# Half of the additions of a softmax denominator as accumulating transfers issued by GpSimd

## The chip, the cores and the metric

The kernel runs on one NeuronCore of a Trainium2 chip. The metric is the time of one execution on the device in microseconds (us), lower being better. Engines are named as in the profile: PE is TensorE (matmuls), PEld its weight loads, DVE is VectorE, ACT is ScalarE, POOL is GpSimd, SP is SyncE, which here only issues transfers.

## The reference

The input x is 8 images of 512 channels by 32 x 32 pixels, float32. Two residual layers follow each other. Layer 1 is a depthwise 3 x 3 convolution, a pruning and a 1 x 1 convolution. Layer 0 holds what the change touches: a 1 x 1 convolution to 2 x 256 channels, then twice (l = 0, 1) a block of a 3 x 3 convolution, an attention over all 1024 pixels and a 1 x 1 convolution, and at the end a 1 x 1 convolution over everything collected. The attention, cut to what matters:

```python
q, k, v = (qkv[:, 0], qkv[:, 1], qkv[:, 2])            # 4 heads of 64 channels, 1024 pixels
logits = jnp.einsum("bhdi,bhdj->bhij", q, k + r) * HD ** (-0.5)
a = jax.nn.softmax(logits, axis=-1)                    # over j
out = jnp.einsum("bhij,bhdj->bhdi", a, v)
```

Softmax needs, for each head and each pixel i, the sum of exp(logits) over the 1024 pixels j.

## The kernel before, in words

**Order of the work.** Images follow each other. Each function adds its pieces to a list under a short name (`add`), and `go` takes them from these lists in the order of a plan, a text of such names: `FIRST` for image 0, `HEAD` and then `TAIL` for images 1 to 6, `HEAD` and then `LAST` for image 7. The two attentions of an image lie in `FIRST` or in `HEAD`. The wrapper `InOrder` keeps that order on PE, DVE, ACT and SP; GpSimd runs its instructions in the order in which they are written too. So each engine has one queue, in the order of the plan, and an instruction that waits holds up everything behind it on its engine. The plans were made by a planner, which is not part of the file.

**One attention** (`attention()`, lines 971 to 1073) has 32 steps: 2 pairs of heads (m), 2 halves of the pixels i (ih), and 8 tiles of 128 pixels j (jt, innermost). The pieces of a step s are

- `s`, scores: 4 small matmuls (8 in the profile, which counts two instructions for each float32 matmul) into a PSUM tile `ps_s` of which there are two;
- `e`, exponentials: ACT writes exp of 128 x 1024 scores to a fresh work tile `e`;
- `w`, values: 4 matmuls of `e` with v, added up over jt in two PSUM banks `ps_av` from a pool of three;
- `p`, add_up: DVE adds `e` to the running tile `sum` of the group (m, ih). The first addition of a group takes two `e` tiles, so 7 additions serve 8 steps.

After the 8 steps of a group, `h` (ACT) copies one bank, and `z` (DVE) adds the other to it, which frees the banks for the next group. After the two groups of one m, `n` multiplies the two `sum` tiles by ones (`ps_dn`, PE), `nr` takes reciprocals (4 pieces on DVE), `ns` spreads them over the partitions by two transfers, and `sc` (DVE) scales z with them. Only then can `m`, the matmuls of the next convolution (`ps_m`), start. The other names that come up below are `Q` (pieces of the last convolution of an image), `o` and `O` (products of the last 1 x 1 convolution of the image before, with `ot` before them and `fr`, `f` behind), `t`, `l`, `lr`, `lp` (its depthwise convolution, activation and pruning; `lp` has an instruction on GpSimd).

**Work tiles.** All `e`, `sum` and many other tiles of 128 x 1024 float32 come from one pool of `NWORK = 11` tiles, used in turn. A tile is given out again when everything that read or wrote it is done; the first writer of its next use waits for that.

The lines that carry the accumulation before the change:

```python
def add_up(s):
    m, ih, jt = steps[s]
    if jt == 1:
        sm[m, ih] = work_tile("sum").rearrange("p (a n) -> p a n", a=2)
    t = flat(sm[m, ih])
    nc.vector.tensor_tensor(t, flat(es[s - 1]) if jt == 1 else t, flat(es[s]), ALU.add)
```

Of the kernel before, what the change touches and what calls it, by code (L numbers as in the profile page):

```python
# [15 lines left out]
P = 128  # L16
# [9 lines left out]
V_N = 396  # L26
LIMIT = 1e20
PITCH = F // 4 + 1
NWORK = 11
NRING = 5  # L30

FIRST_PARTS = [
# [10 lines left out]


FIRST = """
    g*6 gm gd gv g gp g gb gm gd ga gv ga c gp fo gb c ta0 ga ta0 ga ta0 ti0 fo ta2 to0*2 c
    ti0*2 ca ta2*2 c rl ca ta1*3 ti2 ti1 to1 d ti1 d y ya to1 ti1 y ya ti2 to2 d y ti2 d to2 rl
    ya y d*2 ya d P Rc R P d*3 Rc R d*2 P Rc R B P Rc R B*2 P*2 Rc R E Ez B Rc R E Ez k*2 X k dw
    ta0 ka k kp ka ta0*2 v kp ti0 v va ti0 v ti0 q v va ta1 q ta1 qa q*2 qa ta1 s e s e p to0 s
    e p w to0 s e w*2 ti1 s e p ti1*2 p s e p w s to1 s e p w e p w s w to1 ta2 e s e w h p z  # L50
    ta2 s e p ta2 s ti2 e w*2 s e w ti2 to2 ti2 s e w s e to2 w s e w s e w s e rh p w p*5 h z
    s*2 w e*2 n s e w p s p w nr e p w nr*2 s e nc s nr e ns p w s e p w*2 nc s e p w h z s e s
    w s*2 p*2 e w p e*2 p sc p w sc s w e p w s e p w*3 h z n nr*4 ns nc sc Q K m ma sc dp mr
    m*2 ma mr m ma mr ma mr d*4 Q nc K d*3 P d P Rc R d*2 Rc R d*2 P Rc R P*2 Rc B R B P Rc R E
    Ez Rc B*2 R E Ez k X dx k*3 ka*2 kp*2 v*2 q v*2 va*2 cw*3 rk cw q*2 qa q qa s*2 e*2 p s e p
    w s e w s p cw*2 e s e w s e p rk p w s e p*2 s e w s e g*2 w*2 p w h z s e w cw s e p*2
    cw*2 rk s e w*2 s e w s*2 p e rk w p s e g w p g p s*2 e g w g e*2 p w h z p s w e g p w n
    nr s e nr p w g s e s p w nr e s e w p w*2 s nr p e s e w h ns p s e p nc*2 s w e p w s e p
    w s e p w s sc e p s e p w sc w*3 h z n nr*2 Q nr*2 ns z Q sc*2 nc m*2 ma mr ma mr m ma nc m
    ma mr gm mr gd Q gv u A Q x u i A x i gp i*2 Q gb ga*4 Q im id Q iv A Q x ip i*2 ib b bm t*3  # L60
    Q A t x i*2
"""

HEAD = """
    t c*2 t b im id bm c ca iv t ip t l t*2 ib lr b t*3 c bm ca b y d y bm d ya d*2 ya d*3 y P d
    Rc R d*2 P Rc R d P ya d kd Rc R B P Rc R P B*2 Rc R E P Ez Rc B R E Ez y k*3 ya k ka t X lp
    ka t*4 v*2 l t va v*2 va t lr q*2 t*2 lp t q qa s e q qa s e p s t e w t p s e w l p s*2 w
    e*2 p w s p e s w t s w t s e*2 p lr e p w*2 h z s e p w s t w s p s e p e*2 w p s w p e w s
    t e p s w s e w e t p*2 w lp t h z s*2 e p e w s*2 n e*2 w p w s nr s p e w nr e p s e w nr
    s nr t p ns l w e p*2 w lr lp w ot h s e s w p ot s w ot s e*2 p*2 e w p s w e w s e p*2 z  # L70
    sc w nc w*2 h n nc o O nr ok Ok sc z nr*3 ns o ou oa O*2 Ou sc m Oa m sc nc m ma m ma mr ma
    ot mr ma mr o nc mr d ou Ou o O d ou Ou o d O ou*2 oa Ou*2 d Oa o O P d*2 Rc d*3 R P kd d*2
    Rc R d P Rc P R B Rc P B Rc P R B*2 Rc R ou E oa Ou R Oa o O dp E Ez*2 X k v*2 k ou oa Ou
    fr*2 Oa ka fr f*2 fr f*2 dx va k v*2 va k q*2 ka q qa q qa s e s*2 e p e w p s e p w s*2 e*2
    p*2 w s*2 e*2 w*2 s g p e w*2 s e w p s*2 h g e g p w s w z p e*2 s w e g*2 s*2 w*2 p e*2 g
    p*3 g s w*2 e p s e w h s*2 e*2 p z p w*2 s p e p s n w nr*3 w e s g e p w p s e p w*2 s nc
    e nr s ns e nc w s h s p w z w e p s e w s p e*2 p sc s w e p*2 w s sc e p w*3 h n nr*4 ns z
"""

TAIL = """  # L80
# [45 lines left out]
def fast_kernel(  # L126
# [158 lines left out]
    def flat(ps):  # L285
        return ps.rearrange("p n f -> p (n f)")
# [20 lines left out]
    def add(name, *pieces):  # L307
        todo.setdefault(name, []).extend(pieces)
# [662 lines left out]
    def attention():  # L971

        last = HW // P - 1
        steps = [(m, ih, jt) for m in range(2) for ih in range(2) for jt in range(HW // P)]
        pss, es, sm, accs, rs, dns, rr, parts = {}, {}, {}, {}, {}, {}, {}, {}
        quarters = [(r, c) for c in range(2) for r in range(2)]

        def half(r):
            return slice(r * HD, (r + 1) * HD)

        def scores(s):
            m, ih, jt = steps[s]
            ps = pss[s] = big_tile("ps_s")
            for a, c in quarters:
                j = jt * P + c * HD
                nc.tensor.matmul(
                    ps[half(c), a, :],  # L990
                    kr[half(a), m, j : j + HD],
                    qy[half(a), m, ih * 512 : (ih + 1) * 512],
                    start=True,
                    stop=True,
                )

        def exponentials(s):
            e = es[s] = work_tile("e").rearrange("p (a n) -> p a n", a=2)
            nc.scalar.activation(flat(e), flat(pss.pop(s)), AF.Exp, scale=HD ** -0.5)

        def add_up(s):
            m, ih, jt = steps[s]
            if jt == 1:
                sm[m, ih] = work_tile("sum").rearrange("p (a n) -> p a n", a=2)
            t = flat(sm[m, ih])
            nc.vector.tensor_tensor(t, flat(es[s - 1]) if jt == 1 else t, flat(es[s]), ALU.add)

        def values(s):
            m, ih, jt = steps[s]
            if jt == 0:  # L1010
                accs[m, ih] = [bank_tile(f"ps_av{r}") for r in range(2)]
            for r, a in quarters:
                h = 2 * m + a
                nc.tensor.matmul(
                    accs[m, ih][r][half(a), :],
                    vt[half(r), jt, h * HD : (h + 1) * HD],
                    es[s][half(r), a, :],
                    start=(jt == 0),
                    stop=(jt == last),
                )  # L1020

        def part(m, ih):
            t = parts[m, ih] = work_tile("part")[:, :512]
            nc.scalar.copy(t, accs[m, ih][1])

        def join(m, ih):
            zz = z[:, m, ih * 512 : (ih + 1) * 512]
            nc.vector.tensor_tensor(zz, accs[m, ih][0], parts[m, ih], ALU.add)

        def sums(m):  # L1030

            dn = dns[m] = ps_mm.tile([P, 512], F32, tag="mm", name="ps_dn")
            for i in range(4):
                t = sm[m, i // 2]
                nc.tensor.matmul(
                    dn[32 * i : 32 * (i + 1), :], ones, t[:, i % 2, :], start=True, stop=True
                )

        def reciprocal(m, q):
            if q == 0:  # L1040
                rr[m] = work_tile("r")
            c = slice(q * 128, (q + 1) * 128)
            nc.vector.reciprocal(rr[m][:, c], dns[m][:, c])

        def spread(m):

            wide = rs[m] = work_tile("rw")
            for ih in range(2):
                twice = rr[m][half(ih), :512].unsqueeze(1).to_broadcast([HD, 2, 512])
                nc.sync.dma_start(wide[:, ih * 512 : (ih + 1) * 512], twice)  # L1050

        def check(m, src):

            n = rng_used[0]
            rng_used[0] += 1
            src = dns[m] if src == 0 else rr[m][:, :512]
            nc.scalar.activation(rr[m][:, 512:], src, AF.Copy, accum_out=rng[:, n : n + 1])

        def scale(m, ih):
            c = slice(ih * 512, (ih + 1) * 512)  # L1060
            nc.vector.tensor_tensor(z[:, m, c], z[:, m, c], rs[m][:, c], ALU.mult)

        both = [(m, ih) for m in range(2) for ih in range(2)]
        n = len(steps)
        add("s", *[lambda s=s: scores(s) for s in range(n)])
        add("e", *[lambda s=s: exponentials(s) for s in range(n)])
        add("p", *[lambda s=s: add_up(s) for s in range(n) if steps[s][2]])
        add("w", *[lambda s=s: values(s) for s in range(n)])
        add("h", *[lambda m=m, ih=ih: part(m, ih) for m, ih in both])
        add("z", *[lambda m=m, ih=ih: join(m, ih) for m, ih in both])  # L1070
        add("n", *[lambda m=m: sums(m) for m in range(2)])
        add("nr", *[lambda m=m, q=q: reciprocal(m, q) for m in range(2) for q in range(4)])
        add("ns", *[lambda m=m: spread(m) for m in range(2)])
        add("nc", *[lambda m=m, i=i: check(m, i) for m in range(2) for i in range(2)])
        add("sc", *[lambda m=m, ih=ih: scale(m, ih) for m, ih in both])
# [799 lines left out]
```

## Time and profile before

| | before |
|---|---|
| time, median of 2 runs | 2598.15 us (2598.12 to 2598.18) |
| span of the profiled execution | 2595.2 us, granted TensorE clock 0.998 |
| PE busy | 2558.3 us, 99% of the span |
| DVE busy | 2084.2 us, 80% |
| ACT busy | 1185.6 us, 46% |
| POOL busy | 98.0 us, 4% |
| additions of exponentials on DVE | 448 instructions, 553.5 us |
| transfers | 268.49 MB, mean 103 GB/s |

The profile shows one execution. A busy share is an average over the span. The trace shows for each instruction when it started, and what it waited for; matmuls are pipelined, their ends are modelled, so the distance from one start to the next tells more of PE than its busy time.

### The profile page before, as it was taken

Reading aid. Unit: us, or ns where it says so; the run is one execution under the profiler, and the core shown is the slowest. Engines: PE = TensorE matmul, PEld = TensorE weight load, DVE = VectorE, ACT = ScalarE, POOL = GpSimd, SP = SyncE. Lnnn points to the kernel's source line nnn. Section 1 sums busy time; section 2 is a strip of 40 time slices with the busy share of each in tenths; the row PEclk is TensorE's granted clock in tenths of the full one; section 3 lists DMA queues with packets and bytes.
Section 4 is the critical chain, followed back from the end, with each engine's and each line's share of the span. In section 5 each row is a group of like instructions: output and inputs, shape, how many; then the busy total and the mean of one; then the engine's idle time right before and its main releaser. Section 6 shows DMA issues by size and latency. Waiting matters only on the chain.

```text
span 2595.2 us, 36342 instructions
## 1 busy us (share of the span) xinstructions
PE 2558.3 (99%) x14806; PEld 1291.6 (50%) x14806; DVE 2084.2 (80%) x2982; ACT 1185.6 (46%) x1523; POOL 98.0 (4%) x71
## 2 busy tenths in 40 slices
PE   8999999999999999999999999999999999999997
PEld 5454463634636346463464635545355554645443
DVE  8887589877898878887788778887788877888657
ACT  3635436353462544635445344444445444353534
POOL 1000000000000000000000000000000000000000
PEclk9999999999999999999999999999999999999999
DMA  9445230522305113060130602306121151302300
GB/s 349 154 155 203 67 121 25 188 76 73 113 27 213 51 65 122 17 247 17 65 122 17 248 17 80 107 18 246 33 98 73 61 204 33 138 35 96 110 17 34
DMA packets 81773, 268.49 MB, mean 103 GB/s; under 512 B 6848, under 2 KB 37312, under 8 KB 65600
## 3 DMA queue, kind: packets, MB, share of 16 engines
q1 hardware_dynamic: 78048, 262.69, 28.5%
q10 hardware_dynamic: 3552, 3.41, 0.4%
q8 instruction: 118, 1.93, 0.3%
q14 instruction: 55, 0.45, 0.1%
HBM read 212.34 MB, written 36.96 MB: 96 GB/s over the span
## 4 chain that ended last, share of the span: by engine, by line
PE 92%; DVE 4%; ACT 2%; DMA 1%; issue 0%; ACTq 0%; POOL 0%; SPq 0%; DVEq 0%
PE ps_av L105 16%; PE ps_s L105 16%; PE ps_c L105 12%; PE ps_cv L105 11%; PE ps_qk L105 8%; PE ps_cv2q L105 8%; PE ps_q L105 6%; PE ps_v L105 4%; PE ps_m L105 4%; PE ps_y L105 4%; PE ps_dn L105 1%; ACT qy L105 1%; DVE ht L105 1%; DVE vtmp L105 0%; DVE mid L105 0%
## 5 line engine op out<-in xcount | busy, mean ns | idle before, releaser
L105 ACT ACTIVATE e<-ps_s 128x1024 f32<-128x1024 f32 x512 | 509.7, 1023 | 287.1 <-PE ps_s L105 267.4
L105 PE MATMUL ps_s<-qy,kr 64*64 64x512 f32 x4096 | 513.6, 592 | 1.4
L105 DVE TENSOR_TENSOR sum<-sum,e 128x1024 f32<-128x1024 f32 x384 | 475.4, 1238 | 40.2 <-ACT e L105 21.1
L105 PE MATMUL ps_av<-e,vt 64*64 64x512 f32 x4096 | 506.4, 590 | 0.0
L105 DVE SCALAR_TENSOR_TENSOR ht<-xn,v_sb,ht 128x961 f32<-128x961 f32 (+1 forms) x256 | 312.2, 1227 | 8.3 <-ACT ht L105 5.0
L105 PEld LDWEIGHTS ps_s<-qy,kr 64*64 64x64 f32 x4096 | 160.6, 132 | 288.7 <-issue 185.2
L105 PEld LDWEIGHTS ps_av<-e,vt 64*64 64x64 f32 x4096 | 165.8, 133 | 276.9 <-issue 267.6
L105 PE MATMUL ps_qk<-z,wring 128*128 128x512 f32 x512 | 229.7, 596 | 2.0 <-ACT z L105 1.3
L105 DVE TENSOR_TENSOR sum<-e 128x1024 f32<-128x1024 f32 x64 | 78.1, 1221 | 126.2 <-ACT e L105 124.9
L105 ACT COPY c<-ps_c 128x256 f32<-128x256 f32 x96 | 35.6, 370 | 263.4 <-PE ps_c L105 260.2
L105 PEld LDWEIGHTS ps_qk<-z,wring 128*128 128x128 f32 x512 | 95.8, 190 | 118.1 <-issue 99.9
L105 DVE RECIPROCAL r<-ps_dn 128x128 f32<-128x128 f32 x128 | 112.8, 923 | 11.3 <-PE ps_dn L105 9.0
L105 PEld LDWEIGHTS ps_c<-kr,wring 128*128 128x128 f32 x1024 | 116.8, 192 | 8.0 <-issue 7.7
L105 PE MATMUL ps_c<-vt,wring 128*128 128x128 f32 x1024 | 118.1, 276 | 1.8 <-DMA wring<-u 1.1
L105 PE MATMUL ps_c<-qy,wring 128*128 128x128 f32 x1024 | 117.6, 275 | 0.9 <-ACT c L105 0.5
L105 PEld LDWEIGHTS ps_c<-vt,wring 128*128 128x128 f32 x1024 | 116.2, 192 | 2.6 <-ACT c L105 2.1
L105 PE MATMUL ps_cv<-pt,w_sb 128*128 128x512 f32 x256 | 117.3, 609 | 0.0
L105 PE MATMUL ps_c<-kr,wring 128*128 128x128 f32 x1024 | 117.0, 275 | 0.0
L105 PEld LDWEIGHTS ps_c<-qy,wring 128*128 128x128 f32 x1024 | 115.8, 192 | 1.3 <-ACT c L105 0.7
L105 PE MATMUL ps_v<-wring,z 128*128 128x256 f32 x512 | 114.8, 379 | 0.7 <-DVE kr L105 0.7
L105 PE MATMUL ps_m<-z,wm_sb 128*128 128x512 f32 x256 | 112.5, 592 | 0.0
L105 PE MATMUL ps_y<-pt,w_sb 128*128 128x512 f32 x256 | 112.3, 592 | 0.0
(177 smaller groups left out, 3231.2 us busy)
## 6 DMA issues: line engine op xcount, KB each, us to landing
wring<-u SPq DMA_DIRECT2D x96, 1024.0 KB, 4.8
pt<-in_x SPq DMA_DIRECT2D x32, 512.0 KB, 9.6
rw<-r SPq DMA_DIRECT2D x64, 256.0 KB, 3.4
xt<-in_x SPq DMA_DIRECT2D x32, 512.0 KB, 5.9
out<-xt SPq DMA_DIRECT2D x32, 512.0 KB, 3.2
kr<-r SPq DMA_DIRECT2D x14, 1024.0 KB, 6.9
wring<-q SPq DMA_DIRECT2D x14, 896.0 KB, 5.6
wring<-in_wqkv SPq DMA_DIRECT2D x16, 768.0 KB, 4.8
```

Source lines behind the costliest of these rows:

```text
L105: made = method(*args, **kwargs)
```

## The change

Of each attention's 32 steps, the first 28 are taken in pairs (s, s + 1) with s even. For a pair, a new piece `pd` has GpSimd issue a transfer that adds the tile `e` of step s + 1 onto the tile `e` of step s in SBUF; DVE then adds only the even tile to `sum`. The last four steps (28 to 31) are left with one addition each on DVE. So there are 14 transfers and 14 additions in an attention in place of 28 additions. It is for taking half of these additions from DVE. The transfer overwrites tile s, so it waits until `w` of step s has read it, and until `e` of step s + 1 is written. As tiles are held longer, the work pool gets 14 tiles in place of 11[...]. The plans `FIRST` and `HEAD` are new as a whole; `TAIL` and `LAST` are unchanged.

The core of the diff:

```diff
-NWORK = 11
+NWORK = 14
...
+        paired = [s for s in range(0, len(steps), 2) if s < len(steps) - 4]
+        rest = [s for s in range(len(steps)) if s % 2 == 0 or s - 1 not in paired]
+
+        def add_pair(s):
+            nc.gpsimd.dma_start(flat(es[s]), flat(es[s + 1]), accum_op=ALU.add)
+
         def add_up(s):
             m, ih, jt = steps[s]
-            if jt == 1:
+            if jt == 2:
                 sm[m, ih] = work_tile("sum").rearrange("p (a n) -> p a n", a=2)
             t = flat(sm[m, ih])
-            nc.vector.tensor_tensor(t, flat(es[s - 1]) if jt == 1 else t, flat(es[s]), ALU.add)
+            nc.vector.tensor_tensor(t, flat(es[s - 2]) if jt == 2 else t, flat(es[s]), ALU.add)
...
-        add("p", *[lambda s=s: add_up(s) for s in range(n) if steps[s][2]])
+        add("pd", *[lambda s=s: add_pair(s) for s in paired])
+        add("p", *[lambda s=s: add_up(s) for s in rest if steps[s][2]])
...
-    nc = bacc.Bacc("TRN2", target_bir_lowering=False, num_devices=1)
+    nc = bacc.Bacc("TRN2", target_bir_lowering=False, num_devices=1, dynamic_dma_scratch_size=2048)
```

The ends of the attentions in the plans, each up to `n` and a little beyond (old line first, new line second). First attention of `HEAD`, second attention of `HEAD` (there the plan ends), first and second attention of `FIRST`:

```diff
-s w p ot s w ot s e*2 p*2 e w p s w e w s e p*2 z sc w nc w*2 h n nc o O nr ok Ok sc z nr*3 ns
+w p s pd ot e*2 s w pd s e p w s e*2 z sc p*5 w nc w*2 h o n nc O nr ok Ok z nr*3 ns
...
-w z w e p s e w s p e*2 p sc s w e p*2 w s sc e p w*3 h n nr*4 ns z
+w e w*2 p z pd s e s sc s w pd e*2 p e w s sc p e p*4 w*3 h n nr*4 ns z
...
-s w e p w s e p w*3 h z n nr*4 ns nc sc Q K m
+s pd p*3 e p w*2 s e w p w*2 h z Q n nr*4 ns sc nc K m
...
-s sc e p s e p w sc w*3 h z n nr*2 Q nr*2 ns z Q sc*2 nc m*2
+s sc e s e w sc w p*5 w*2 h z Q n nr*4 ns z Q sc*2 nc m*2
```

## The prediction, made before the run

> **What bounds the kernel now.** First the page: busy shares, and the chain of work that ended last.
>
> ```profile
> PE 2558.3 (99%) x14806; PEld 1291.6 (50%) x14806; DVE 2084.2 (80%) x2982; ACT 1185.6 (46%) x1523; POOL 98.0 (4%) x71
> PE 92%; DVE 4%; ACT 2%; DMA 1%; issue 0%; ACTq 0%; POOL 0%; SPq 0%; DVEq 0%
> ```
>
> PE is the limit, and DVE, which the change relieves, is not. Busy PE could still be slow PE, so I took the distances between starts from the timeline: 8 small matmuls (one `s` or `w`) take 0.86 us, 0.107 each.
>
> ```profile
> 1040.23 1.04 PE L105 MATMUL ps_s<-qy,kr 64*64 64x512 f32 x8
> 1041.09 1.90 PE L105 MATMUL ps_av<-e,vt 64*64 64x512 f32 x16
> ```
>
> In the same way the chain gives 0.429 us for a 128x512 matmul (16 in 6.87), 0.112 for 128x128 (192 in 21.44), 0.216 for 128x256 (16 in 3.45). With the counts of the groups: 8192 x 0.107 + 2664 x 0.429 + 3072 x 0.112 + 512 x 0.216 = 2474, and some 30 for `ps_dn` and the group sums: PE needs about 2504 us of the 2595. At most 91 us (3.5%) can be won by anything that leaves the matmuls alone. Where are they? Windows over the 317 us of one middle image have PE busy in all but 0.25 us:
>
> ```profile
> sum 317.00, PE 316.75 PEld 160.39 DVE 258.38 ACT 145.41 POOL 10.71; mean PE 18.63 PEld 9.43 DVE 15.20 ACT 8.55 POOL 0.63
> ```
>
> In the list of waits, what PE loses to DVE's additions is 0.4 us in all; its longest wait is in the first 8 us of the kernel. DVE in turn waits in these additions for the exponentials:
>
> ```profile
> PE pm L105 <- DVE mv L105: 9.1, 2, 8.0
> PE ps_dn L105 <- DVE sum L105: 0.4, 1, 0.4
> DVE sum L105 <- ACT e L105: 146.0, 87, 8.9
> ```
>
> So there is next to nothing to win inside an image. What can be lost is read at the ends of the attentions, where PE comes to `n` and needs the sums. First attention of a `HEAD` (DVE, PE), then the second:
>
> ```profile
> 1077.87 6.53 DVE L105 TENSOR_TENSOR sum<-sum,e 128x1024 f32<-128x1024 f32 x5
> 1080.08 1.04 PE L105 MATMUL ps_s<-qy,kr 64*64 64x512 f32 x8
> 1083.62 1.89 PE L105 MATMUL ps_dn<-sum,ones 128*32 128x512 f32 x8
> 1094.12 3.17 PE L105 MATMUL ps_m<-z,wm_sb 128*128 128x512 f32 x7
> 1212.50 1.04 PE L105 MATMUL ps_s<-qy,kr 64*64 64x512 f32 x8
> 1214.66 1.23 DVE L105 TENSOR_TENSOR sum<-sum,e 128x1024 f32<-128x1024 f32 x1 [0.23 <-ACT e L105]
> 1216.04 1.07 PE L105 MATMUL ps_dn<-sum,ones 128*32 128x512 f32 x8
> ```
>
> The last addition ends at 1084.3 and 1215.9, which is 4.2 and 3.4 us after the last `s` (step 31) starts, and `n` follows at once. There is no slack here: whatever delays the last sum delays PE. After the first, `ps_m` comes 10.5 us behind `n` with only 9 us of other matmuls between: reciprocals, `rw` transfer and scaling are on the path too.
>
> [...]
>
> **The change part by part.**
>
> Removed: 14 of 28 additions in each of 16 attentions, 224 x 1.238 us = 277 us of DVE (80% to 70%):
>
> ```profile
> L105 DVE TENSOR_TENSOR sum<-sum,e 128x1024 f32<-128x1024 f32 x384 | 475.4, 1238 | 40.2 <-ACT e L105 21.1
> ```
>
> Worth 0: they lie beside PE, which waited 0.4 us for them.
>
> Added: 224 transfers. The latency L of one, from its last input to the release of DVE, is not in the trace.
>
> ```profile
> wring<-u SPq DMA_DIRECT2D x96, 1024.0 KB, 4.8
> kr<-r SPq DMA_DIRECT2D x14, 1024.0 KB, 6.9
> out<-xt SPq DMA_DIRECT2D x32, 512.0 KB, 3.2
> ```
>
> Low end 3.2 (as a plain copy of the same size); high end 6.9 (the slower 1 MB row[...]). [...] the last two transfers of an attention are issued 1.7 us apart[...]. I take **L = 5.5**.
>
> In mid-attention L is hidden. Walking the new plan with 0.86 us per `s` and `w`, the transfer of pair (4, 5) of the first `HEAD` attention can start 7.7 us before `z`, which the next group's banks need about 1.7 us later; before `z` stand one addition on it and `z` itself, 1.9 us. That holds to L of about 7. Behind a waiting `pd`, GpSimd's queue holds only other `pd`, prunings (1.8 us each, the last due at `ot` some 5 us after its place) and the small powers of the normalizations, which come after the attention. Fourteen tiles give a tile back some 17 to 20 us after it is taken, against e, `w`, L and addition of about 12: hidden.
>
> At the ends it isn't hidden. In both `HEAD` attentions, from the end of `w` of step 26, which releases the last transfer, to the start of step 31's `s` there are 5 pieces on PE, 4.3 us. DVE's queue then holds five additions: that of pair (26, 27), and behind it, in order, steps 28 to 31. They end L + 5 x 1.24 = L + 6.2 after the release, thus L + 1.9 after the last `s` starts. Before it was 4.2 and 3.4. The loss is L - 2.3 in the first attention (the `o` that the plan puts ahead of `n` only moves filler, for the path n to `ps_m` is critical there) and L - 1.5 in the second, where the plan ends and nothing fills: 3.2 + 4.0 = 7.2 us. Seven images run `HEAD`: **50 us**.
>
> `FIRST` puts a `Q` ahead of `n`, which hides the late sums but takes filler from behind `n`. Before:
>
> ```profile
> 142.52 1.04 PE L105 MATMUL ps_s<-qy,kr 64*64 64x512 f32 x8
> 146.06 1.07 PE L105 MATMUL ps_dn<-sum,ones 128*32 128x512 f32 x8
> 154.03 6.17 PE L105 MATMUL ps_m<-z,wm_sb 128*128 128x512 f32 x14
> ```
>
> From the last `s` to `ps_m` 11.5 us, of which n to `ps_m` 8.0. Now `s`, three `w` (3.4), `Q` (16 x 0.43 = 6.9), then the 8.0 with PE empty: 18.3, loss 6.8. In the second attention (s at 266.3, n 270.7, `ps_m` 281.0, 14.7 in all) it becomes 4.3 + 5.2 (`Q`, 12 matmuls) + 8.5 = 18.0, loss 3.3. Together **10 us**.
>
> The new start (a `y` ahead of the `c`): same matmuls, and the second `P` waited for its weights (1.1 us), not for these; 0, +-2. [...] Sum: 7 x (2L - 3.8) + 10 = 14L - 17 = 60 us at L = 5.5: 2598 + 60 = **2658**.
>
> **The rivals.**
>
> A. All hidden: the sums arrive as before because L is near 3 or the release comes earlier than I walk it, and the relieved DVE pays the rest. For it: DVE has 30% free, and only the last transfer matters. Against it: five additions stand behind it. At L = 3.2 the sum is 28 us, 2626; with no loss at all 2598. This one is not slower by over 2%.
>
> B. The transfers are slow[...]. At L = 9 the ends cost 14 x 9 - 17 = 109, and `z` waits at two group ends of an attention, 1.5 us each by the walk above: 16 x 2 x 1.5 = 48. That gives 2755. For it: no adding transfer has been seen here. Against it: [...] DMA is 9 to 24% busy in the four attention windows that I looked at.
>
> C. Faster: DVE's relief removes small stalls. The bound is 91 us[...]; 0.4 us hangs on the sums. At best some 5 us: 2593.
>
> **How the numbers follow.** Forecast [...] 0.62; A 0.22; B 0.14; C 0.02. 2% slower begins at 2650, which is L = 4.9: about 0.7 of the forecast, and B, make 0.57 slower; faster by 2% would need half of all PE slack, 0.01; the rest, 0.42, is within 2%. Range: from 2612, which cuts off half of A and C, to 2705, which cuts off most of B.
>
> **What would show it.** Right: PE waiting in `ps_dn` for `sum`, some 4 us at the second attention of each of seven images, and for `z` before `ps_m`; DVE idle in `sum` waiting for the transfer on `e`; the landing time gives L. An idle gap of about 7 us before `ps_m` near 155 us shows the `FIRST` step. Wrong: `ps_dn` without waits (A), or scores waiting on exponentials and `ps_av` on `z` in mid-attention (B).

## The result, and the profile after

The changed kernel takes 2729.95 us (two runs, 2727.55 to 2732.34) against 2598.15: a ratio of 1.0507, 95% interval 1.0462 to 1.0552. It is slower by 132 us, on the side that was forecast and by more than twice the amount (60 us, range to 2705).

The page of the changed kernel, busy shares, the chain of work that ended last, and what the change added:

```profile
PE 2611.4 (96%) x14806; PEld 1323.7 (48%) x14806; DVE 1825.8 (67%) x2758; ACT 1184.1 (43%) x1523; POOL 288.1 (11%) x295
...
PE 84%; DMA 7%; DVE 6%; ACT 2%; issue 1%; SPq 0%; ACTq 0%; DVEq 0%; POOL 0%; POOLq 0%
...
L1006 POOL DMA_DIRECT2D e<-e x224 | 194.1, 867 | 1235.2 <-ACT e L105 970.9
...
L105 DVE TENSOR_TENSOR sum<-sum,e 128x1024 f32<-128x1024 f32 x160 | 197.7, 1236 | 62.3 <-DMA e<-e 54.9
...
e<-e POOLq DMA_DIRECT2D x224, 512.0 KB, 4.9
```

DVE lost 258 us of work, as meant. None of it shows in the time. PE does the same 14806 matmuls, but busy plus idle changed: idle from 37 to 119 us, and PE's own busy time from 2558 to 2611, so that its matmuls also ran slower. The chain now has 7% of transfers and 6% of DVE in it. The list of waits of the same run (us in total, times, longest) says where PE stood:

```profile
PE ps_dn L105 <- DVE sum L105: 51.6, 16, 4.7
PE ps_s L105 <- ACT e L105: 15.6, 12, 5.6
PE ps_m L105 <- DVE z L105: 7.8, 2, 6.5
...
DVE sum L105 <- DMA e<-e: 370.1, 86, 17.5
```

The 0.4 us that PE waited for sums has become 51.6, at 16 places: both attention ends of images 1 to 7, and in image 0 the `n` in the middle of the first attention and the one at the end of the second. Read one of them, the second attention of an image with `HEAD`, in the timeline. First GpSimd, then DVE, then PE:

```profile
1285.23 0.86 POOL L1006 DMA_DIRECT2D e<-e  x1 [0.86 <-PE ps_av L105]
```
```profile
1291.57 1.23 DVE L105 TENSOR_TENSOR sum<-e 128x1024 f32<-128x1024 f32 x1 [3.05 <-DMA e<-e]
1292.90 3.88 DVE L105 TENSOR_TENSOR sum<-sum,e 128x1024 f32<-128x1024 f32 x3
1297.24 1.23 DVE L105 TENSOR_TENSOR sum<-sum,e 128x1024 f32<-128x1024 f32 x1 [0.46 <-DVE sum L105]
```
```profile
1289.23 1.04 PE L105 MATMUL ps_s<-qy,kr 64*64 64x512 f32 x8
1290.09 2.75 PE L105 MATMUL ps_av<-e,vt 64*64 64x512 f32 x24
1292.77 1.05 PE L105 MATMUL ps_dn<-sum,ones 128*32 128x512 f32 x4
1298.52 1.84 PE L105 MATMUL ps_dn<-sum,ones 128*32 128x512 f32 x4 [4.70 <-DVE sum L105]
...
1311.56 4.88 PE L105 MATMUL ps_m<-z,wm_sb 128*128 128x512 f32 x11
```

The chain of waits gives the pieces:

```profile
1282.03 2.62 PE ps_av L105 x24
...
1285.23 6.25 DMA e<-e
...
1291.57 1.24 DVE sum L105
```

`w` of step 26 ends at 1284.65, the transfer starts at 1285.23 and takes 6.25, DVE starts at 1291.57. So L is 6.92 us here. The five additions depend on each other and take 6.91 (five of 1.24, and the handing over between them). They end 9.2 us after the last `s` begins, where it was 3.4; `ps_m` comes after 22.3 instead of 14.9.

There is a second thing in these lines. The four `ps_dn` behind the wait take 1.84 us where the four ahead of it took 1.05. The windows over the same stretch show why (PEclk is the figure before the last two):

```profile
1290.00:1295.00 5.00, 3.82 (x32) 0.91 (x24) 3.22 (x3) 1.61 (x2) 0.00 (x0) 1.00 0.03 6
1295.00:1300.00 5.00, 1.48 (x4) 0.14 (x4) 2.91 (x3) 0.00 (x0) 0.00 (x0) 0.87 0.02 5
1300.00:1305.00 5.00, 5.00 (x11) 2.17 (x10) 4.60 (x7) 0.00 (x0) 0.00 (x0) 0.79 0.00 0
```

The clock granted to PE falls to half after the gap, for 3.4 us: it is 0.50 in each us from 1299 to 1302, and 1.00 again from 1303 on. In the records of the clock the kernel before has 9 us at half clock within its span, all in its last 26 us. The changed one has 101 us: 20 stretches of 3.4 or 6.8 us at gaps of PE, and 8.5 us at its end. After the first 20 us, all 13 gaps of more than 3.3 us (by the modelled ends of the matmuls) had such a stretch at their end, beginning from 3.2 us before PE's next matmul to 1.4 us after it; so had 7 of the 8 gaps from 2.0 to 3.3 us, the shortest of them 2.04 us, and none of the 7 from 1 to 2 us.

Image 0, which runs `FIRST`, lost some 47 us by itself in this profile: the first `s` of image 1 starts at 438.49 us, before at 391.46. Its two attentions take 53 and 54 us from the first to the last `s` before, 71 and 70 after. Windows over them, before and after:

```profile
89.00:143.00 54.00, 53.92 (x497) 18.43 (x500) 47.83 (x48) 42.75 (x51) 0.00 (x0) 1.00 0.49 169
212.00:267.00 55.00, 54.49 (x489) 20.89 (x492) 49.96 (x55) 34.35 (x39) 0.00 (x0) 1.00 0.50 163
```
```profile
88.00:160.00 72.00, 62.85 (x500) 20.00 (x504) 30.34 (x33) 42.88 (x52) 12.40 (x14) 0.93 0.89 235
239.00:310.00 71.00, 60.90 (x490) 19.59 (x492) 33.07 (x40) 34.19 (x39) 12.23 (x14) 0.93 0.88 219
```

The DMA engines (the last figure but one) were half busy with the preparation of weights before a single pair was added; with the transfers they are busy 0.89 of the time. The issues of the stretch from 90 to 345 us show what that does to both sides (KB each, median us to landing), before and after:

```profile
u<-uplane SPq DMA_DIRECT2D x12, 256.0 KB, 3.4
...
s<-scomb SPq DMA_DIRECT2D x8, 256.0 KB, 4.3
```
```profile
e<-e POOLq DMA_DIRECT2D x28, 512.0 KB, 7.1
...
u<-uplane SPq DMA_DIRECT2D x12, 256.0 KB, 7.8
...
s<-scomb SPq DMA_DIRECT2D x8, 256.0 KB, 10.2
```

The weights' tiles `uplane` and `scomb` come from the same pool of work tiles as the exponentials. A transfer that lands late gives its tile back late, the exponential behind it waits for a tile, and PE for the exponential. ACT's waits in the first and in the second of these attentions show it:

```profile
ACT e L105 <- DMA u<-uplane: 6.7, 3, 3.9
...
ACT e L105 <- DMA s<-scomb: 12.0, 2, 7.4
```

In the kernel before, all instructions on tiles `e` together waited 1.7 and 1.5 us for these two. PE's waits for exponentials in image 0 went from nothing that its list shows to 13.6 us.

### The profile page after: what moved, and what is told of

Its sections match the earlier page's. It is cut to its first block, busy times and chain, and to the rows that moved or that the text cites. A ratio compares the mean times of both kernels' runs of the same rounds, so it can differ in the third digit from the quotient of the medians.

```text
span 2730.5 us, 36599 instructions
## 1 busy us (share of the span) xinstructions
PE 2611.4 (96%) x14806; PEld 1323.7 (48%) x14806; DVE 1825.8 (67%) x2758; ACT 1184.1 (43%) x1523; POOL 288.1 (11%) x295
## 4 chain that ended last, share of the span: by engine, by line
PE 84%; DMA 7%; DVE 6%; ACT 2%; issue 1%; SPq 0%; ACTq 0%; DVEq 0%; POOL 0%; POOLq 0%
PE ps_s L105 13%; PE ps_av L105 13%; PE ps_c L105 11%; PE ps_cv L105 11%; PE ps_cv2q L105 8%; PE ps_qk L105 8%; PE ps_q L105 5%; PE ps_m L105 4%; PE ps_v L105 4%; PE ps_y L105 4%; DMA e<-e 3%; DVE sum L105 3%; PE ps_dn L105 1%; DMA ht<-in_w 1%; DMA wring<-u 1%
## 5 line engine op out<-in xcount | busy, mean ns | idle before, releaser
L105 ACT ACTIVATE e<-ps_s 128x1024 f32<-128x1024 f32 x512 | 508.0, 1023 | 323.2 <-PE ps_s L105 286.3
L105 PE MATMUL ps_s<-qy,kr 64*64 64x512 f32 x4096 | 522.5, 599 | 18.6 <-ACT e L105 15.6
L105 PE MATMUL ps_av<-e,vt 64*64 64x512 f32 x4096 | 510.8, 592 | 1.8 <-ACT part L105 1.8
L1006 POOL DMA_DIRECT2D e<-e x224 | 194.1, 867 | 1235.2 <-ACT e L105 970.9
L105 DVE SCALAR_TENSOR_TENSOR ht<-xn,v_sb,ht 128x961 f32<-128x961 f32 (+1 forms) x256 | 318.2, 1251 | 8.8 <-ACT ht L105 5.0
L105 PEld LDWEIGHTS ps_s<-qy,kr 64*64 64x64 f32 x4096 | 167.6, 133 | 308.7 <-issue 159.2
L105 PEld LDWEIGHTS ps_av<-e,vt 64*64 64x64 f32 x4096 | 182.9, 134 | 265.9 <-issue 229.0
L105 DVE TENSOR_TENSOR sum<-e 128x1024 f32<-128x1024 f32 x64 | 80.2, 1254 | 320.8 <-DMA e<-e 315.2
L105 DVE TENSOR_TENSOR sum<-sum,e 128x1024 f32<-128x1024 f32 x160 | 197.7, 1236 | 62.3 <-DMA e<-e 54.9
L105 PE MATMUL ps_qk<-z,wring 128*128 128x512 f32 x512 | 229.7, 595 | 3.4 <-ACT z L105 2.2
L105 DVE RECIPROCAL r<-ps_dn 128x128 f32<-128x128 f32 x128 | 111.2, 920 | 94.2 <-PE ps_dn L105 93.3
L105 PEld LDWEIGHTS ps_qk<-z,wring 128*128 128x128 f32 x512 | 95.7, 190 | 119.0 <-issue 99.0
L105 ACT COPY c<-ps_c 128x256 f32<-128x256 f32 x96 | 35.5, 370 | 262.3 <-PE ps_c L105 259.1
L105 PE MATMUL ps_m<-z,wm_sb 128*128 128x512 f32 x256 | 114.9, 601 | 7.8 <-DVE z L105 7.8
L105 PEld LDWEIGHTS ps_c<-kr,wring 128*128 128x128 f32 x1024 | 116.8, 192 | 7.9 <-issue 7.9
L105 PE MATMUL ps_c<-vt,wring 128*128 128x128 f32 x1024 | 117.5, 275 | 3.2 <-DMA wring<-u 2.5
L105 PE MATMUL ps_c<-qy,wring 128*128 128x128 f32 x1024 | 117.7, 275 | 1.7 <-DMA wring<-u 1.6
L105 PEld LDWEIGHTS ps_c<-vt,wring 128*128 128x128 f32 x1024 | 115.9, 192 | 3.6 <-issue 2.6
L105 PE MATMUL ps_c<-kr,wring 128*128 128x128 f32 x1024 | 117.0, 275 | 0.0
L105 PEld LDWEIGHTS ps_c<-qy,wring 128*128 128x128 f32 x1024 | 115.8, 192 | 2.2 <-ACT c L105 1.9
L105 PE MATMUL ps_v<-wring,z 128*128 128x256 f32 x512 | 114.8, 379 | 0.7 <-DVE kr L105 0.7
L105 PE MATMUL ps_y<-pt,w_sb 128*128 128x512 f32 x256 | 115.0, 603 | 0.0
```

The costliest lines, as they stand in the source:

```text
L105: made = method(*args, **kwargs)
L1006: nc.gpsimd.dma_start(flat(es[s]), flat(es[s + 1]), accum_op=ALU.add)
```

## The experiments

Eleven kernels. Each time stands beside runs of the kernel before on the same chip, whose medians were 2597.6 to 2598.5. L105, the line of a helper, moves with the edits.

**The last pairs moved behind the last steps.** In images 1 to 7 the last group of a sum takes steps 28 to 31 first and the two transferred pairs last:

```diff
...
+        else:
+            add("p", *[lambda i=i, s=s: add_up(s, i) for i, s in enumerate((29, 30, 31, 24, 26))])
```

> In images 1 to 7 the last group's five additions are taken in the order 28+29, 30, 31, 24, 26 in place of 24+26, 28, 29, 30, 31, so that the additions that need no transfer don't stand behind one; plans and transfers as in the changed kernel. Theory (at the ends of the attentions PE waits for sums that stand behind the last transfer): the last sum ends about 6 us after the last scores start, in place of 8.0 to 10.0; some 2.5 to 3 us come back at 14 ends, and part of the half-clock stretches behind them: 2670 to 2695. Rival (the transfers slow the whole attention, by load on the DMA engines or by tiles given back late): no more than 5 us come back, 2725.

Measured: 2670.56 us, ratio 1.028 (1.0263 to 1.0297). In this kernel the last sum begins anew with the pairs, so that steps 28 to 31 are left out of it; the additions are as many, and the run below with both edits has them all. As theory had it: 59 us are given back when the additions no longer stand behind the transfer. In the timeline of the same attention end, the wait is 1.29 in place of 4.70 us, and no half clock follows:

```profile
1265.81 1.04 PE L105 MATMUL ps_s<-qy,kr 64*64 64x512 f32 x8
...
1271.69 1.05 PE L105 MATMUL ps_dn<-sum,ones 128*32 128x512 f32 x4 [1.29 <-DVE sum L105]
...
1283.08 7.03 PE L105 MATMUL ps_m<-z,wm_sb 128*128 128x512 f32 x16
```

**Work for PE while it waits.** Three matmuls that nobody reads at the first attention end of images 1 to 7, five at the second, into the bank that `n` then overwrites:

```diff
             dn = dns[m] = ps_mm.tile([P, 512], F32, tag="mm", name="ps_dn")
+            if m and not first:
+                for _ in range((3, 5)[l]):
+                    nc.tensor.matmul(dn, g_sb, qy[:, 0, :512], start=True, stop=True)
```

> Changed kernel with 3 (first attention) and 5 (second attention of an image) useless 128x128x512 matmuls ahead of the ones-matmuls of images 1 to 7, written to the bank that these then overwrite: PE has something to do while it waits, and the sums end as late as before. Theory (an idle PE of 3 to 5 us is followed by 3.4 or 6.8 us at half clock, which costs 1.7 us and more at each second attention's end): the half-clock stretches of images 1 to 7 are gone and the time falls, by 10 to 25 us, to 2705 to 2720, although PE does 48 us more of work. Rival (the half clock is only a reading of the idle time and costs nothing): no change, or longer by what doesn't fit into the wait, 2730 to 2740.

Measured: 2706.93 us, ratio 1.0426 (1.0409 to 1.0444), 23 us less than the changed kernel though PE has 56 matmuls more. The time at half clock falls from 101 to 37 us, and what is left lies in image 0 and in the tail. The same attention end:

```profile
1279.80 1.04 PE L105 MATMUL ps_s<-qy,kr 64*64 64x512 f32 x8
...
1283.34 4.56 PE L105 MATMUL ps_dn<-qy,g_sb 128*128 128x512 f32 x10
...
1289.71 1.05 PE L105 MATMUL ps_dn<-sum,ones 128*32 128x512 f32 x4 [0.82 <-DVE sum L105]
...
1301.09 7.03 PE L105 MATMUL ps_m<-z,wm_sb 128*128 128x512 f32 x16
```

The sums come no earlier than in the changed kernel (the last four `ps_dn` start 9.9 us after the last `s`, there 9.3), but the four `ps_dn` take 1.05 us again and the matmuls up to `ps_m` run at full clock. So 23 us were the clock's.

**Image 0 as before.** Its old plan, no transfers in it, the rest as changed:

```diff
-        paired = [s for s in range(0, len(steps), 2) if s < len(steps) - 4]
+        paired = [s for s in range(0, len(steps), 2) if s < len(steps) - 4 and not first]
```

> Image 0 with the plan of before and no transfers, images 1 to 7 as in the changed kernel. Theory (the first image lost 47 us of the 132, from transfers that share the DMA engines with the stores and loads of its weight preparation, and from its plan): 2680 to 2688. Rival (the first image costs only the 10 us that the prediction gave its plan, the rest is lost in images 1 to 7): about 2720.

Measured: 2684.14 us, ratio 1.0332 (1.0314 to 1.0349): image 0 costs 46 us, the other seven 86.

**The pairs by DVE.** The plans of the change, the transfer's work done by an addition at its place:

```diff
-            nc.gpsimd.dma_start(flat(es[s]), flat(es[s + 1]), accum_op=ALU.add)
+            nc.vector.tensor_tensor(flat(es[s]), flat(es[s]), flat(es[s + 1]), ALU.add)
```

> The changed kernel, plans and tiles, with each pair added by DVE in place of a transfer, at the same place of the plan: 28 additions on DVE again. Theory (what costs is the latency of the transfers and their load on the DMA engines, and the plan costs some 10 us in the first image): 2600 to 2620, and no half clock at the ends of images 1 to 7. Rival (the new order of the work itself is slower): 2650 and more.

Measured: 2693.73 us, ratio 1.0367 (1.035 to 1.0385). That is far off what was expected, and the waits say why:

```profile
DVE e L105 <- PE ps_av L105: 186.7, 93, 11.2
```

A pair may be added only when `w` has read its first half, so the addition waits for PE; on GpSimd's queue that wait (169.4 us in the changed kernel) holds up little else, on DVE's it holds up every addition behind it. For the attention ends this run decides nothing. For image 0 it says more, though the additions stand on DVE's queue there too: without transfers, but with the new plan, its last `ps_m` begins 16 us later than before, where the change makes it 46. The DMA engines are busy 0.48 and 0.46 of its two attentions, as before. Some 30 us of image 0 go with the transfers.

**Tiles alone.** The kernel before with `NWORK = 14` and `dynamic_dma_scratch_size=2048`:

> The kernel before with fourteen work tiles in place of eleven [...], and nothing else. Theory: neither costs time, 2598, within 4 us. Rival: the three more tiles move a work tile's addresses or the order of releases, and carry part of the 132 us; then 2605 or more.

Measured: 2595.93 us, ratio 0.999 (0.9983 to 0.9997). Neither is a cost.

**Both edits.** Image 0 as before, and in images 1 to 7 the last group in the order 28 to 31, then pairs, with all steps in the sum:

> The changed kernel with two edits at once: image 0 by the plan of before without transfers, and in images 1 to 7 the last group's additions in the order steps 28 to 31 first, then the sums of the two transferred pairs. Theory: the two losses are separate, so the savings add: 2730 less 46 (image 0) less 59 (pair last) is 2625, within 10 us, and nothing is left of the half clock at the ends of images 1 to 7. What is left of the loss, some 27 us, is the last pair's transfer at the second attention's end, 2 to 3 us in each of 7 images. Rival: the two edits cure the same loss, as it would be if the transfers loaded the whole kernel; then 2645 or more.

Measured: 2628.58 us, ratio 1.0117 (1.01 to 1.0134). The savings add, within 4 us: the two losses are separate. Against the run with image 0 as before, the order of the additions is worth 56 us here, with every step in the sum. The mean clock is 0.997 again, and half of the 30 us that are left is in one line of its waits:

```profile
PE ps_dn L106 <- DVE sum L106: 14.9, 15, 1.4
```

From the last `s` to `ps_m` the first ends take 1.0 us longer than before and the second ones 2.5.

**Transfers in the early groups only.** The plans of before, pairs in the first of the two groups of each sum, each transfer at the place of the addition that it replaces (`plain` is image 0, without transfers in the first of two runs and with them in the second):

```diff
+        paired = [] if plain else [0, 2, 4, 6, 16, 18, 20, 22]
```

> Plans and order of the kernel before, with fourteen tiles; in images 1 to 7 the transfers add the pairs of the first of the two groups of eight steps of each sum vector, m = 0 and m = 1 (8 transfers and 8 additions fewer on the VectorE for an attention, 112 transfers in all), each used by the VectorE 3 to 6 us later; the second group, after which the normalization comes, is added by the VectorE alone. Image 0 has no transfers. Theory: a transfer costs time only at an attention's end, so 2598, within 5 us, while the VectorE has some 110 us less work. Rival 1: the transfers load the exponentials' tiles or the DMA engines in mid-attention, then 2610 or more. Rival 2: the relief of the VectorE is worth something once nothing waits at the ends, then 2590 or less.

> The same as the run of early pairs, with the same transfers in image 0 too (16 more), on the plan of before. It asks what the load of the transfers on the DMA engines does in image 0, where weights are prepared by other transfers, without the plan's shift of the piece ahead of the normalization. Theory: the load was some 29 us with 28 transfers, so 10 to 20 us over the run of early pairs, with the transfers of uplane and scomb landing late. Rival: image 0 lost by the plan and by waits at its attentions' ends alone, then within 4 us of the run of early pairs.

Measured: 3003.15 and 3061.74 us (ratios 1.1545 and 1.1794). Neither question was answered, because the plan of before has an addition ahead of the `w` that reads its tile. There the transfer stood in front of `w`: the values were multiplied with summed exponentials, and PE waited for the transfers. The first of the two, PE's waits:

```profile
PE ps_av L105 <- DMA e<-e: 290.0, 75, 7.6
```

The granted clock fell to 0.953 as well. 405 us for 112 transfers is 3.6 us of PE for each: that was the price, in this run, of a transfer that stands ahead of the last reader of its target.

**The same, behind `w`.** Transfers behind the `w` that reads their target, results used three `w` later:

> Plans and order of the kernel before, with fourteen tiles; in images 1 to 7 the transfers add the pairs of the first of the two groups of eight steps of each sum vector (112 transfers in all). Each is placed right behind the value matmuls that read its target, and the VectorE takes its result three pieces of value matmuls later; the second group, after which the normalization comes, is added by the VectorE alone. Image 0 has no transfers. Theory: a transfer costs time only at an attention's end, so 2598, within 5 us, while the VectorE has some 110 us less work. Rival 1: the transfers load the exponentials' tiles or the DMA engines in mid-attention, then 2610 or more. Rival 2: the relief of the VectorE is worth something once nothing waits at the ends, then 2590 or less.

Measured: 2621.47 us, ratio 1.0088 (1.0075 to 1.0102), by the letter the first rival. The trace puts the time elsewhere than in the transfers, which land after a median of 4.7 us. PE's waits:

```profile
PE ps_dn L115 <- DVE sum L115: 7.7, 8, 1.5
PE ps_s L115 <- ACT e L115: 7.3, 7, 1.8
```

`ps_m` comes 0.6 to 1.7 us later at the first attention ends and 1.0 at the second: some 15 of the 23 us. The other 8 are in the first attentions themselves, where PE waits for exponentials. The additions taken three `w` later fall into the second group, which before had only its own; that this is the cause is not shown, and the last run below speaks against it as the whole of it.

**The same in image 0.**

> The same as the run of early transfers behind the value matmuls, with the same transfers in image 0 too (16 more), on the plan of before. It asks what the load of the transfers on the DMA engines does in image 0, where weights are prepared by other transfers, without the plan's shift of the piece ahead of the normalization. Theory: the load was some 29 us with 28 transfers, so 10 to 20 us over the run without them in image 0, with the transfers of uplane and scomb landing late. Rival: image 0 lost by the plan and by waits at its attentions' ends alone, then within 4 us of that run.

Measured: 2645.55 us, ratio 1.018 (1.0166 to 1.0194), 24 us over the preceding run, for 16 transfers and the plan of before. Windows over its two attentions show the load again, 0.74 and 0.79 in place of 0.48 and 0.51 in the run without them:

```profile
89.00:153.00 64.00, 55.74 (x493) 18.07 (x496) 33.48 (x33) 42.32 (x51) 7.17 (x8) 0.95 0.74 207
228.00:290.00 62.00, 56.43 (x478) 18.77 (x480) 40.20 (x46) 33.70 (x38) 6.99 (x8) 0.94 0.79 212
```

The transfers alone, without the shifted `Q`, stretch the attentions of image 0, by 19 of the 24 us from the first to the last `s`; `uplane` lands after 4.4 us in place of 2.6, `scomb` after 7.1 in place of 4.5. That it is more than the 10 to 20 expected for 16 transfers says that the loss doesn't go by their number.

**Results taken within their group.** Pairs 0, 2, 16 and 18 only; DVE adds steps 4 and 5, then 6, pair 0, step 7, pair 2:

```diff
+        paired = [] if plain else [0, 2, 16, 18]
+LATE = [5, 6, 0, 7, 2, 9, 10, 11, 12, 13, 14, 15, 21, 22, 16, 23, 18, 25, 26, 27, 28, 29, 30, 31]
```

> As the run of early transfers behind the value matmuls, image 0 without transfers, but with the pairs of steps 0, 2, 16 and 18 alone (4 transfers for an attention, 56 in all), and the VectorE takes their results within the same group of eight steps, as its last additions but one or so; so no addition moves into the second group. It asks whether the 23 us of that run came of additions that moved into the second group, where the VectorE is nearly full and the normalization comes next, or of the transfers themselves. Theory: the former, so 2598, within 5 us. Rival: each transfer costs a bit wherever it stands (23 us for 112 is 0.2 us each), so 2609 or more.

Measured: 2617.9 us, ratio 1.0077 (1.0063 to 1.0091). Theory missed again: with half as many transfers almost the same is lost. So it isn't 0.2 us for each transfer either. From the first `s` to the last, the first attention of `HEAD` takes 55.17 us, as before; the loss is at its end, where the sums are ready 5.84 us after the last `s` in place of 4.33. DVE's timeline of that attention:

```profile
1064.00 0.68 DVE L105 TENSOR_TENSOR z<-ps_av,part 128x512 f32<-128x512 f32 x1
1067.92 1.77 DVE L105 RECIPROCAL r<-ps_dn 128x128 f32<-128x128 f32 x2 [3.23 <-PE ps_dn L105]
1069.60 1.16 DVE L105 TENSOR_TENSOR sum<-e 128x1024 f32<-128x1024 f32 x1
...
1073.39 5.06 DVE L105 TENSOR_TENSOR sum<-sum,e 128x1024 f32<-128x1024 f32 x4
...
1082.86 1.23 DVE L105 TENSOR_TENSOR pt<-ht,pt 128x1024 f32<-128x1024 f32 x1 [0.94 <-POOL ht L615]
...
1085.14 6.54 DVE L105 TENSOR_TENSOR sum<-sum,e 128x1024 f32<-128x1024 f32 x5
```

The additions that went were the early ones of the group. In their place DVE stands still 3.2 us with nothing that it could do, then has the remaining ones in a bunch, and comes to the last five 1.5 us later than before, counted from the last `s`. The wait of 0.94 us for a pruning (`ht`, GpSimd) explains little of that: DVE is 1.4 us late ahead of it. In the second attention the last four `s` come 0.8 to 1.3 us late; there PE waits for `part` ahead of `ps_av`. That the holes are the cause is read from the trace; no run took them away by themselves.

No version with transfers beat the kernel before.

## Why the prediction was wrong

**Right.** PE bounds the kernel, and DVE's relief is worth nothing: 258 us of it went and no run shows a gain. The last transfer of an attention stands ahead of five dependent additions, and the sums that come late hold PE in `ps_dn`; it was forecast at "some 4 us at the second attention", and is 4.70 in the lines above, 3.4 to 4.7 in the seven images. Moving the pair behind the other additions took 59 us away, so this cause is shown. Mid-attention is hidden in images 1 to 7: from 345 us on PE waits 2.0 us in all for exponentials. The trace of the change also has hardly slower additions for the traffic (1236 ns against 1238; the first of each group 1254 against 1221). Of the rivals, A (hidden) is out, and of B's signs the stalls of scores in mid-attention show in image 0 alone; there `ps_av` waited 1.8 us too, for `part`.

**The term "7 x (2L - 3.8)", 50 us, was mis-sized.** It measures 86 (image 0 as before leaves that much). Two things are in the difference. L was taken as 5.5, an estimate between the 3.2 and 6.9 us of transfers that don't add; at the fourteen ends it is 6.0 to 7.6, in the mean 6.5, at the upper end of its range and beyond. The median landing of all 224 is 4.9, but the last of an attention, issued 1.7 us behind the one before it, as the prediction had it, lands after 5.3 to 6.9 at these ends. With L = 6.5 the same formula gives 64. The other 22 or so are the clock: the filler took 23 us away, and with it images 1 to 7 lose 62. The prediction had the gap of 4 us and did not ask what PE does after it: here the granted clock is half for 3.4 or 6.8 us, of which at most 1.1 lie inside the gap. Both kinds of ends pay for that. From the last `s` to `ps_m` the first ones take 4.9 us more than before in the mean and the second ones 7.0; with filler it is 2.9 and 5.3.

**The step "`FIRST` ... Together 10 us" failed.** It was right for the ends that it looked at: the gap ahead of `ps_m` was forecast as "about 7 us" and is 6.5 (at 178.88 us), and the second attention's end lost 2.6 where 3.3 was worked out. But image 0 lost 46. Some 30 of these are inside its attentions, 71 and 70 us long in place of 53 and 54 (3.4 us of that are eight matmul instructions of `ps_qk`, which the new plan puts into the first of them). One of the waits there, 3.36 us at 141.57 us, is at the `n` in the middle of the first attention, which the prediction did not look at. The prediction dismissed load with "DMA is 9 to 24% busy in the four attention windows that I looked at". All four were in images 1 and 3. In image 0 the same column reads 0.49, and the walk by which L was hidden, with fourteen tiles given back in time, did not hold there. Two runs bear it out: without transfers the new plan costs image 0 some 16 us (the pairs added by DVE), and with the old plan 16 transfers cost it 24. So what failed is the load of the transfers in image 0, which the prediction put at nothing on windows of other images.

The sum is 86 + 46 = 132.

**What stays open.** The share of image 0's loss that goes over late tiles was not separated by a run from that of the half clock after the gaps; by the clock of 0.93 in the windows above, the second is at most some 10 us inside its attentions. Nor was a version tried that gives DVE its early additions back and takes away others.

## What to carry to other kernels

Before work is moved to a slower path because an engine has less to do afterwards, look where in the schedule its relief falls: where the last run took early additions off DVE, it stood still for 3.2 us in their place, and came to the last five, on which the next stage hangs, 1.5 us later than before. Check a resource that a change loads (here the DMA engines) in the stage where it is busiest (0.49 in image 0 before the change, 0.89 after), not in a typical one. And price a wait on PE as the gap plus what comes after it: in the changed kernel all 13 gaps of more than 3.3 us, and 7 of the 8 from 2.0 to 3.3 us, had 3.4 or 6.8 us at half the clock at their end.

## What the runs showed of the hardware

- In the changed kernel an adding transfer from work tile to work tile (512 KB) lands after 4.4 us at the least, 4.9 in the median and 12.9 at the most. Its packets of 4096 bytes take 328 ns in the median; plain ones of that size on the queue of SP take 159.
- From its issue to its first packet pass 1.4 to 1.5 us in most of the 33 cases where no other was under way, and GpSimd is busy 0.87 us for one. Of L = 6.92 in the example above, 0.58 pass before the issue. A transfer's own packets, 128 of 4096 bytes at 328 ns, are 2.6 us if they divide evenly over 16 engines: an estimate. The rest was not split up; the transfer issued 1.72 us earlier moves its data in the same stretch, in which the DMA share is 0.98 or more in each us from 1285 to 1290.
- 23 of 132 us were given back by matmuls whose results nobody reads.
